# A graph network on one core: TensorE's filler products are removed and their PSUM bank is given to the layers

## The chip, the core and the metric

The kernel runs on one core of one Trainium2 chip. A core has five engines that run their own instruction streams: TensorE (PE in the profile; its weight loads are PEld), VectorE (DVE), ScalarE (ACT), GpSimd (POOL) and the sync engine (SP), which here only issues transfers. TensorE writes its results to PSUM, of which the program uses eight banks of 128 x 512 fp32. The metric is the device time of one execution in microseconds, the median of several runs.

## The reference

Sixteen graphs of 1024 nodes with 64 features each. `adj` holds a weight for each pair of neighbours (about nine a node) and zeros elsewhere. Four layers follow each other, each on the normalised and rectified features, each added to `x`:

```python
h = jnp.maximum(_layernorm(x, axis=-1), 0.0)
x = x + _L0_gnn_ref(h, adj, L0_gnn_W)      # (adj @ h) @ W.T
h = jnp.maximum(_layernorm(x, axis=-1), 0.0)
x = x + _L1_gnn_ref(h, adj, ...)           # two dense layers, adj @ m, then a GRU cell
h = jnp.maximum(_layernorm(x, axis=-1), 0.0)
x = x + _L2_gnn_ref(h, adj, ...)           # K0 h + K1 adj h + K2 (2 adj adj h - h), then dense
h = jnp.maximum(_layernorm(x, axis=-1), 0.0)
x = x + _L3_gnn_ref(h, adj, nodemask, ...) # weighted quantiles over the neighbours, then two dense layers
```

The last layer drops some neighbours of nodes that have more than ten ("dilation"), and takes, for each node and feature, three weighted and interpolated quantiles of the values of the neighbours that are left.

## The kernel before, in words

The program is written by a planner at build time, `Weave` (L311). The work is divided into chains, Python generators that yield one operation at a time. An operation (`Op`, L248) names its engine, the places that it reads and writes, and a reckoned cost (`Line.cost`, L291). `Weave.run` (L415) keeps a reckoned time for each engine, looks at the next operation of each chain, and issues the one that can start first; among those that can start within `SLACK` of it, the chain with the lowest key goes first. The order so found is fixed for each engine (`behind`, L441). Nothing is decided at run time: an engine works through its list, and each instruction waits for the semaphores of what it depends on. The line of nearly all instructions in the profile is therefore that of the helper, L288; gathers have L613, stores L619, scatters L1245.

Each gather on GpSimd is moreover tied to TensorE (`leash`, L394 to L400): it waits for the last of those products that another engine has waited for and that end, by the reckoning, before the gather starts.

The chains are:

- `listing` (L626): loads rows of `adj` and finds each node's neighbours on VectorE (MAX8 and MATCH_REPLACE8 over `key` and `cand`).
- `transposing` (L798): loads blocks of `adj`, turns them on TensorE into the two banks of stock `tp` (`bank<-c,block`), and ScalarE copies them to `AT`. Fifteen `AT` tiles exist.
- `layering` (L1037), twice: two lanes, one for even and one for odd graphs, go through layers 0 to 2 (`layers`, L851). A lane holds one `pay` tile with its graph's features, and takes PSUM banks from stock `fm`, at most two at a time: one while features are multiplied by the adjacency (`bank<-AT,nodes`), a second where the result of the step before is still in use (L921 to L933, L984 to L1008). Products with 64-column weights and 512-column data are two to a pass. At the end a graph's features and lists are stored to HBM (`table`, `rows`).
- `gathering` (L1043): GpSimd fetches, for each graph, 10 x 8 tiles of neighbours' features with indirect DMAs (80 gathers of 128 rows) into one of two `G` tiles. After the 16 graphs come four lists of nodes with many neighbours (`MANY`, L51), picked from all graphs: 22, 28, 48 and 24 gathers.
- `quantiling` (L1072) and `dense` (L1185): VectorE sorts the gathered values with a network of minima and maxima over `G` and `net`, and weighs them (`G<-G,coef`); TensorE sums the weighed cells in a bank of stock `q` (`bank<-G,c`), and goes through the last two dense layers (`bank<-c,yo`, `bank<-of_h,m`, `bank<-m,h`), with ScalarE between them; VectorE masks and adds (`yo<-bank,pay`).

Banks 0 and 1 are stock `tp`, 2 and 3 stock `q`, 4 to 6 stock `fm` (L569 to L571). A stock is a queue: the bank given back longest ago is taken next. Bank 7 belongs to no stock. It takes the products of constants (L565 to L568): a tile of ones, 128 x 128, times ones, 128 x 512, in fp16, whose result nobody reads. When `run` is about to issue an operation on TensorE, and the engine's reckoned idle time before it is over 0.5 us, it first issues as many of these as fill nine tenths of that time at 0.22 us each (L434 to L437). In the built program there are 2705 of them in 223 bursts, each with a weight load of its own. They stand in TensorE's list between the real products, and wait for nothing.

Of the kernel before, what the change touches and what calls it, by code (L numbers as in the profile page):

```python
# [22 lines left out]
P = 128  # L23
# [75 lines left out]
EXTRA = 6 * NT  # L99
BIG = 1e30  # L100
SLACK = 0.1
FILL = 0.9
GATHER = 1.33
RANK = 3.0
SHARE = 3
# [34 lines left out]
def progressions(s):  # L140

    found, top = [], max(s) + 1
    for st in sorted(s):
        found.append((frozenset([st]), (st, 0, 1, 0, 1)))
        for d in range(1, top):
            run = [st]
            while run[-1] + d in s:
                run.append(run[-1] + d)
                found.append((frozenset(run), (st, 0, 1, d, len(run))))
                for e in range(d * (len(run) - 1) + 1, top):  # L150
                    both, k = list(run), 1
                    while all(x + k * e in s for x in run):
                        both += [x + k * e for x in run]
                        k += 1
                        found.append((frozenset(both), (st, e, k, d, len(run))))
    return found
# [56 lines left out]
def fast_constants():  # L213

    k, m = np.arange(P)[:, None], np.arange(P)[None, :]
    r = np.arange(-(NT - 1) * P, N)[None, :]
    half = {
        "keys": ((N - r) * (r != k)),
        "since": (k < m) - 1.0,
        "iota": np.broadcast_to(m, (P, P)),  # L220
        "ordinal": np.broadcast_to(1 + np.arange(LIST)[None, :], (P, LIST)),
    }
    kmax = max(n for _, n in MANY)
    whole = {
        "ident": (k == m),
        "quarter": 0.25 * (k == m),
        "node": P * np.arange(NT)[None, :] + k,
        "shift": np.broadcast_to(P * np.arange(NT)[None, :], (P, NT)),
        "bins": np.broadcast_to(np.array([LONG]), (P, BINS)),
        **{f"place{n}": np.broadcast_to(np.array([order]), (P, len(order))) for n, (_, order) in SORTED.items()},  # L230
        "graph": np.broadcast_to(N * np.arange(GRAPHS)[None, :], (P, GRAPHS)),
        "place": np.broadcast_to(np.arange(kmax)[None, :], (P, kmax)),
        "taus": np.broadcast_to(np.array([TAUS[0], TAUS[1], TAUS[1], TAUS[2]])[None, :], (P, 4)),
    }

    whole["room"] = np.array([[P * sum(t for t, n in MANY if n > many) if many else GRAPHS * N for many in LONG]])
    tables = []
    for parts, dtype in ((half, np.float16), (whole, np.float32)):
        at, cols = {}, 0
        for name, a in parts.items():  # L240
            at[name] = (cols, a.shape[1])
            cols += a.shape[1]
        tables += [np.concatenate([np.broadcast_to(a, (P, a.shape[1])).astype(dtype)
                                   for a in parts.values()], axis=1), at]
    return tables


class Op:  # L248
# [5 lines left out]
    def __init__(self, line, make, writes, reads, cost, later=0.0, after=()):  # L254
        self.line, self.make, self.cost, self.later, self.after = line, make, cost, later, after
        self.writes, self.reads = [place(a) for a in writes], [place(a) for a in reads]
# [54 lines left out]
class Weave:  # L311
# [6 lines left out]
    def __init__(self, tc):  # L318
        self.tc = tc
        self.free, self.past, self.last, self.stocks, self.chains = {}, {}, {}, {}, []  # L320
        self.ends, self.time, self.free_pairs, self.count = {}, 0.0, set(), 0
        self.spare = self.leash = None
        self.awaited, self.made = [], {}

    def stock(self, name, tiles):
# [89 lines left out]
    def run(self):  # L415
        while True:
            before = None
            while before != (before := [(id(c["want"]), id(c["op"])) for c in self.chains]):
                for chain in sorted(self.chains, key=lambda c: c["key"]):
                    if not self.advance(chain):  # L420
                        self.chains.remove(chain)
            heads = [c for c in self.chains if c["op"]]
            if not heads:
                break
            best = {}
            for c in heads:
                op = c["op"]
                c["start"] = max(self.free.get(op.line, 0.0), op.ready)
                best[op.line] = min(best.get(op.line, 1e9), c["start"])
            line = min(best, key=best.get)  # L430
            chain = min((c for c in heads if c["op"].line is line and c["start"] <= best[line] + SLACK),
                        key=lambda c: c["key"])
            op, start = chain["op"], chain["start"]
            if self.spare and line is self.spare[0]:  # L434
                gap = start - self.free.get(line, 0.0)
                for _ in range(int(FILL * gap / self.spare[4]) if gap > 0.5 else 0):
                    self.issue(Op(line, self.spare[1], *self.spare[2:4], self.spare[4]), self.free.get(line, 0.0), ("spare", 0))  # L437
            chain["op"], chain["value"] = None, self.issue(op, start, (chain["gen"].__name__, chain["key"]))
        assert not self.chains, [c["want"] for c in self.chains]

# [14 lines left out]
class Fast:  # L455
# [4 lines left out]
    def __init__(self, tc, half, whole, weights):  # L460
        self.tc, self.nc = tc, tc.nc
        (W0, W1, b1, W2, b2, Wih, bih, Whh, bhh, Wc, K, bc, M1, mb1, M2, mb2) = weights
        nc = self.nc
# [7 lines left out]
        _, at16, _, at32 = fast_constants()  # L471
# [88 lines left out]
        def stock(name, count, shape, dtype=F32):  # L560
            weave.stock(name, [p.tile(shape, dtype, name=f"{name}{i}") for i in range(count)])

        banks = [ps.tile([P, 512], F32, name=f"bank{i}") for i in range(8)]
        self.bank = banks[0]
        busy = banks[7]  # L565
        ones = self.ones16
        weave.spare = (self.T, lambda: nc.tensor.matmul(busy, ones[:, 0:P], ones[:, 0:512], start=True, stop=True),  # L567
                       [busy], [ones], 0.22)  # L568
        weave.stock("tp", banks[0:2])  # L569
        weave.stock("q", banks[2:4])  # L570
        weave.stock("fm", banks[4:7])  # L571


        stock("row", 2, [P, N])
# [1327 lines left out]
```

## Time and profile before

| | |
|---|---|
| median of 3 runs | 2494.44 us (2476.52 to 2508.35) |
| the profiled execution's own time | 2479.22 us |
| its span, first to last instruction | 2477.4 us |
| TensorE's mean granted clock | 0.882 of full speed |
| products (and weight loads) on TensorE | 8704, of which 2705 of constants |
| busy time of the constants' products | 676.4 us |
| gathers on GpSimd | 1402, mean 1.116 us |
| first gather, last gather's end | 152.1 us, 2411.2 us |

A row of the page's groups reads: line, engine, operation, out<-in by the program's names, shapes, count, then busy time and mean ns of one, then the idle time of the engine just before such instructions and what ended it. An fp32 product stands in the trace as two records. A row of the chain gives the share of the span that an engine or a line has on the way back from the last instruction. Rows of stretches give their start and end, the length, each engine's busy time with the number of instructions, the granted clock of TensorE, the share of the DMA engines and GB/s. A row of the timeline gives start, length, engine, line, operation and, in brackets, the idle time before it and what ended it.

### The profile page before, as it was taken

Reading aid. Unit: us, or ns where it says so; the run is one execution under the profiler, and the core shown is the slowest. Engines: PE = TensorE matmul, PEld = TensorE weight load, DVE = VectorE, ACT = ScalarE, POOL = GpSimd, SP = SyncE. Lnnn points to the kernel's source line nnn. Section 1 sums busy time; section 2 is a strip of 40 time slices with the busy share of each in tenths; the row PEclk is TensorE's granted clock in tenths of the full one; section 3 lists DMA queues with packets and bytes.
Section 4 is the critical chain, followed back from the end, with each engine's and each line's share of the span. In section 5 each row is a group of like instructions: output and inputs, shape, how many; then the busy total and the mean of one; then the engine's idle time right before and its main releaser. Section 6 shows DMA issues by size and latency. Waiting matters only on the chain.

```text
span 2477.4 us, 28435 instructions
## 1 busy us (share of the span) xinstructions
PE 2168.9 (88%) x8704; PEld 955.1 (39%) x8704; DVE 1796.3 (73%) x4505; ACT 935.2 (38%) x2714; POOL 1595.6 (64%) x1441
## 2 busy tenths in 40 slices
PE   8999899999898979897988898989898887779857
PEld 3344334343443333434342434342433333334414
DVE  5878687878696878787878877887777484447553
ACT  4444444354444353535353535353534211101000
POOL 1037676767675767676766676776676677777670
PEclk9999898889897989898989898999897887889969
DMA  6345526262626262616252525262522112121110
GB/s 211 111 112 155 115 65 136 57 138 64 121 74 137 56 160 49 149 39 155 56 133 53 139 65 134 60 146 49 140 38 36 23 35 27 23 28 29 23 24 5
DMA packets 265406, 208.68 MB, mean 84 GB/s; under 512 B 78208, under 2 KB 225984, under 8 KB 265248
## 3 DMA queue, kind: packets, MB, share of 16 engines
q1 hardware_dynamic: 218368, 157.32, 23.3%
q0 software_dynamic: 46096, 48.62, 13.0%
q8 instruction: 72, 1.18, 0.2%
q10 hardware_dynamic: 784, 0.86, 0.1%
q14 instruction: 86, 0.70, 0.1%
HBM read 187.51 MB, written 19.17 MB: 83 GB/s over the span
## 4 chain that ended last, share of the span: by engine, by line
PE 61%; DVE 14%; issue 7%; another core or an unknown queue 7%; ACT 7%; DMA 3%; POOL 1%; SPq 0%; ACTq 0%; DVEq 0%; POOLq 0%
PE bank L288 49%; PE bank L567 13%; DVE G L288 5%; DVE net L288 3%; ACT sq L288 2%; DVE cand L288 1%; DMA block<-in_adj 1%; ACT wide L288 1%; DVE hn L288 1%; DMA pay<-in_x 1%; ACT nodes L288 1%; ACT G L288 1%; DVE st L288 1%; DVE pay L288 1%
## 5 line engine op out<-in xcount | busy, mean ns | idle before, releaser
L613 POOL DMA_INDIRECT G<-table,pay x1402 | 1564.9, 1116 | 812.9 <-issue 374.3
L567 PE MATMUL bank<-ones 128*128 128x512 f16 x2705 | 676.4, 399 | 57.4 <-issue 55.7
L288 PE MATMUL bank<-AT,nodes 128*64 128x512 f32 x2048 | 645.9, 650 | 38.8 <-ACT nodes L288 21.2
L567 PEld LDWEIGHTS <-ones 128*128 128x128 f16 x2705 | 267.6, 102 | 412.6 <-issue 162.8
L288 PEld LDWEIGHTS bank<-AT,nodes 128*64 128x64 f32 x2048 | 171.5, 146 | 374.8 <-issue 286.3
L288 ACT ACTIVATE sq<-pay,st 128x64 f32<-128x64 f32 x512 | 177.1, 346 | 130.1 <-DVE st L288 65.5
L288 DVE MAX8 cand<-key 128x8 f16<-128x128 f16 x1024 | 214.4, 279 | 5.7 <-DVE key L288 2.1
L288 ACT ACTIVATE AT<-bank 128x512 f32<-128x512 f32 x256 | 148.3, 591 | 177.5 <-PE bank L288 131.1
L288 ACT ACTIVATE wide<-bank 64x512 f32<-64x512 f32 x128 | 75.6, 591 | 359.8 <-PE bank L288 253.6
L288 PE MATMUL bank<-c,block 128*128 128x128 f32 x976 | 185.7, 313 | 21.1 <-ACT AT L288 9.1
L288 DVE TENSOR_TENSOR G<-G 128x1024 f32<-128x1024 f32 (+7 forms) x215 | 187.2, 903 | 2.6
L288 PEld LDWEIGHTS bank<-c,block 128*128 128x128 f32 x976 | 127.5, 158 | 159.4 <-issue 135.5
L288 DVE SCALAR_TENSOR_TENSOR key<-row,c 128x1024 f16<-128x1024 f32 x124 | 150.2, 1211 | 38.0 <-DMA row<-in_adj 29.3
L288 PE MATMUL bank<-G,c 128*128 128x512 f32 (+3 forms) x382 | 165.0, 571 | 14.0 <-DVE G L288 7.1
L288 ACT ACTIVATE nodes<-pay,off,ri 128x64 f32<-128x64 f32 x384 | 148.8, 430 | 36.1 <-DVE off L288 15.8
L288 DVE TENSOR_TENSOR yo<-bank,pay 128x256 f32<-128x256 f32 (+2 forms) x36 | 14.8, 411 | 181.5 <-PE bank L288 97.6
L288 DVE TENSOR_TENSOR net<-G 128x1024 f32<-128x1024 f32 (+7 forms) x140 | 141.1, 1033 | 1.3
L288 ACT ACTIVATE G<-G,coef 128x64 f32<-128x64 f32 x384 | 93.8, 336 | 96.8 <-DVE coef L288 96.7
L288 DVE TENSOR_TENSOR G<-net 128x512 f32<-128x512 f32 (+12 forms) x123 | 110.2, 939 | 1.2
L288 DVE MAX8 L<-cand 128x8 f16<-128x64 f16 x384 | 87.4, 228 | 29.2 <-remote 9.7
L288 PE MATMUL bank<-wide,wg 64*64 64x512 f32 (+1 forms) x192 | 105.1, 628 | 3.6 <-ACT wide L288 3.4
L288 DVE TENSOR_TENSOR G<-G,net 128x1024 f32<-128x1024 f32 (+5 forms) x113 | 104.4, 960 | 1.4
(176 smaller groups left out, 2238.4 us busy)
## 6 DMA issues: line engine op xcount, KB each, us to landing
row<-in_adj SPq DMA_DIRECT2D x124, 512.0 KB
block<-in_adj SPq DMA_DIRECT2D x122, 512.0 KB
G<-table,pay POOLq DMA_INDIRECT x1402
rows<-pay SPq DMA_DIRECT2D x16, 632.0 KB
G<-in_adj SPq DMA_DIRECT2D x10, 512.0 KB
table<-pay SPq DMA_DIRECT2D x16, 264.0 KB
pay<-in_x SPq DMA_DIRECT2D x16, 256.0 KB
out<-yo SPq DMA_DIRECT2D x16, 256.0 KB
```

The costliest lines, as they stand in the source:

```text
L288: return Op(self, lambda: f(*args, **kwargs), writes, reads, cost, later)
L567: weave.spare = (self.T, lambda: nc.tensor.matmul(busy, ones[:, 0:P], ones[:, 0:512], start=True, stop=True), [busy], [ones], 0.22)
L613: return self.nc.gpsimd.indirect_dma_start(out=out, out_offset=None, in_=table, in_offset=bass.IndirectOffsetOnAxis(ap=at, axis=0))
```

## The change

The block in `run` that issues products of constants goes, with its constant `FILL` and its attribute `spare`. The bank that took their results is the fourth of stock `fm`. Nothing else is changed; the order of the rest is found anew by the same planner.

```diff
-FILL = 0.9
...
-        self.spare = self.leash = None
+        self.leash = None
...
             op, start = chain["op"], chain["start"]
-            if self.spare and line is self.spare[0]:
-                gap = start - self.free.get(line, 0.0)
-                for _ in range(int(FILL * gap / self.spare[4]) if gap > 0.5 else 0):
-                    self.issue(Op(line, self.spare[1], *self.spare[2:4], self.spare[4]), self.free.get(line, 0.0), ("spare", 0))
             chain["op"], chain["value"] = None, self.issue(op, start, (chain["gen"].__name__, chain["key"]))
...
         self.bank = banks[0]
-        busy = banks[7]
-        ones = self.ones16
-        weave.spare = (self.T, lambda: nc.tensor.matmul(busy, ones[:, 0:P], ones[:, 0:512], start=True, stop=True),
-                       [busy], [ones], 0.22)
         weave.stock("tp", banks[0:2])
         weave.stock("q", banks[2:4])
-        weave.stock("fm", banks[4:7])
+        weave.stock("fm", banks[4:8])
```

## The prediction

> **What bounds the kernel now.** I read the page first (busy shares, clock, chain), then the stretches by stage, the waits, and at the end the timeline of the places that they point to. From the page:
>
> ```profile
> PE 2168.9 (88%) x8704; PEld 955.1 (39%) x8704; DVE 1796.3 (73%) x4505; ACT 935.2 (38%) x2714; POOL 1595.6 (64%) x1441
> ...
> PEclk9999898889897989898989898999897887889969
> ...
> PE 61%; DVE 14%; issue 7%; another core or an unknown queue 7%; ACT 7%; DMA 3%; POOL 1%; SPq 0%; ACTq 0%; DVEq 0%; POOLq 0%
> ...
> L613 POOL DMA_INDIRECT G<-table,pay x1402 | 1564.9, 1116 | 812.9 <-issue 374.3
> L567 PE MATMUL bank<-ones 128*128 128x512 f16 x2705 | 676.4, 399 | 57.4 <-issue 55.7
> ```
>
> TensorE is busiest and holds 61% of the chain that ended last, but 676.4 of its 2168.9 us are the products of constants (L567). Real products take 1492 us, 60% of the span. GpSimd's gathers are the second candidate: a gather and its issue cost 1.116 + 0.30 us, so the 80 of one graph 113 us.
>
> By stage (first gather at 152 us, last graph's layers done near 1955), all engines, then the constants alone. Columns: stretch, its length, then PE, PEld, DVE and so on, the granted clock last but two.
>
> ```profile
> 152.00:1955.00 1803.00, 1621.74 (x6424) 713.48 (x6424) 1386.52 (x3546) 801.43 (x2333) 1245.32 (x1120) 0.88 0.42 96
> 1955.00:2477.40 522.40, 409.32 (x1668) 181.69 (x1668) 298.06 (x501) 61.15 (x182) 338.66 (x300) 0.86 0.14 24
> ```
>
> ```profile
> 152.00:1955.00 1803.00, 357.55 (x1400) 138.55 (x1400) 2.23 (x2) 0.88 0.42 96
> 1955.00:2477.40 522.40, 278.08 (x1132) 111.86 (x1132) 0.00 (x0) 0.86 0.14 24
> ```
>
> In the layers' stage real products take 1264 us of 1803, at a mean clock of 0.88. The chain of waits cut to this stage gives 56.6% to real products (1020 us) and 6.9% to constants (124 us). In the tail constants are two thirds of PE's work. The clock in steps of 3 us around one of the longer waits (length, PE busy, clock):
>
> ```profile
> 651.00:654.00 3.00, 2.38 (x8) 1.00 1.19 257
> 654.00:657.00 3.00, 0.00 (x0) 0.80 0.84 172
> 657.00:660.00 3.00, 1.55 (x2) 0.50 1.20 227
> 660.00:663.00 3.00, 3.00 (x13) 0.50 0.82 108
> 666.00:669.00 3.00, 3.00 (x10) 0.50 0.41 64
> 669.00:672.00 3.00, 3.00 (x16) 0.92 0.63 150
> ```
>
> The reader sees what a gap costs: 3 to 4 us without a product, and the clock is halved for 13 us, nine of them full of real work. Stepping through the whole stage so, I count 56 such falls, 433 us at half clock, 7.7 us each. Nearly every 3.4 us with less than about a third of its time in streaming products is followed by a fall, and the clock comes back only after a nearly solid one.
>
> Waits (total, times, longest):
>
> ```profile
> POOL G L613 <- PE bank L288: 161.7, 132, 10.3
> DVE yo L288 <- PE bank L288: 97.6, 23, 23.7
> ```
>
> The gathers wait for real products of PE, since each is tied to the products that the planner puts before it: PE sets the pace of the stage and GpSimd follows close behind. The 23.7 us lies near the end, in the timeline:
>
> ```profile
> 2406.18 2.96 DVE L288 TENSOR_TENSOR G<-G,coef 128x1024 f32<-128x1024 f32 x3
> 2407.49 32.82 PE L567 MATMUL bank<-ones 128*128 128x512 f16 x145 [0.82 <-issue]
> 2439.94 4.29 PEld L288 LDWEIGHTS bank<-G,c 128*128 128x128 f32 x20
> 2450.17 0.42 DVE L288 TENSOR_TENSOR yo<-bank,pay 128x256 f32<-128x256 f32 x1 [23.68 <-PE bank L288]
> ```
>
> The weighted cells are ready at 2409.1, but PE works through constants until 2440.
>
> **What the skill says.** The Trainium skill, "TensorE: Matmul & The Clock Gate", Part 1, "What's actually happening": the array's clock has two states, half and full; an idle window of about 3.4 us brings half, a busy one gives full back. The trace agrees (0.50 and 1.00 above), with one difference: stretches without a gap but thin in work, as at 604 to 614 us, fall too. The same page, "Why this matters for your kernels", advises no PE gap over about 3 us; the constants do that. "PSUM — Partial Sum Buffer", Terms, counts eight banks; the program names eight, and the constants' one is free once they go. "Perfetto Trace Analysis" calls TensorE's end times modelled, so I use start-to-start spacing: 246 constants in 54.16 us, 0.22 us each.
>
> **The change part by part.**
>
> *The fourth bank.* In the built programs the order of TensorE's instructions, constants and bank numbers left out, is the same for the first 2400 of some 3980 rows, and after that only neighbours change places. So the stock of three hardly ever ran empty, and the planner's order barely moves. TensorE's waits on ScalarE fall from 854 to 827, GpSimd's on TensorE from 550 to 544. PE's waits for ScalarE's `wide` are about 1 us each (27.3 us, 27 times), so 27 of them are 27 us at the very most, and most stand where PE waits anyway. Bounds: -20 us to +5 us (a swap that puts a late product first). I take 0.
>
> *Relief: real work no longer queued behind constants.* Upper bound in the stage: constants on the chain, 124 us. Lower bound: I set the first real weight load after each of the 166 bursts against the last semaphore event that it waits for; the delays sum to 75 us, of which 1020/1264 = 0.81 is on the chain, 61 us. I take -100, nearer the top, because the last event is often later than the one needed. Head (0 to 152): 8.4% of the chain is 13 us at most, 7 by the events; I take -9.
>
> *Loss: a colder clock.* The stage's 166 bursts: 25 have 16 products or more (3.4 us and up), 20 have 7 to 15, 121 fewer. I let each long one give one more cold stretch of real work, and every second middle one: 25 + 10 = 35, at 7.7/2 = 3.9 us lost each, 136 us of PE, 0.81 of it on the chain: +110. The short ones I put at nothing: the products around them keep the window full. If that cover fails for one in four, it is 30 stretches more, 95 us on the chain. If half of the long bursts end in a fall already today (constants at half clock are seen: 55 of 345 us), it is 55 us less. Head: 4 long and 2 middle bursts, (4 + 1) x 3.9 x 0.85: +17. In the head the clock is 0.98, so it has most to lose.
>
> *The tail.* From 1955 to 2411 the gathers run nearly without a break, so most constants there lie in real waits, and cost nothing. Three places do. The 23.68 us above goes: the products start at 2409 instead of 2440, take 10 us at full clock and some 18 at half, and are done at 2427, as VectorE gets there (2426.5); about 1 us stays. A gather's wait of 5.85 us at 2334.8, for cells that PE frees late after a burst at 2304 to 2326, goes for 5. The last chain of products (2459 to 2466) is colder: +5. Sum -23.7 + 1 - 5 + 5, about -22. Next late after that is VectorE's network itself.
>
> *Instruction supply.* 5410 of PE's 17408 instructions go. In 2366 to 2407 constants came one in 0.7 us multiples with nothing to wait for. Not priced, bounds 0 to -15.
>
> *Sum.* Head -9 + 17, stage -100 + 110, tail -22: -4 us. Against the execution's own 2479.22 that is 2475. The median shown, 2494.44, is 15 above it; on its footing I say 2490.
>
> **The rivals.**
>
> *Slower: the clock decides.* Real work in the stage is 1264 x 0.88 = 1112 us at full clock. At a mean clock c it takes 1112/c. At c = 0.75 that is 1483, +219, on the chain +177; less relief 100 and tail 22, plus head 10: +65, so 2560. It decides from c = 0.79 down, where 0.81 x (1112/c - 1264) eats the other 114. For it: the thin stretches that fall without any gap. Against: without constants PE's load is 70%, and a half-clocked PE fills its windows with backlog, which brings the clock back.
>
> *Faster: PE regains slack.* Today nine tenths of every reckoned gap are filled, so a PE that is late after a cold stretch cannot catch up, and gathers wait. Full relief 124 + 13, half the loss (55 + 9), tail 22: -95, so 2400. For it: 161.7 us of gathers waiting for PE. Against: the longest such waits (10.3 us at 1944.8, 5.6 at 921) have no or few constants in the 20 us before; PE is full of real work at half clock there.
>
> *The bank does not act,* as above: no time of its own, within the likeliest case.
>
> **How the numbers follow.** Relief and loss balance: 0.46, own range 2445 to 2540. Slower rival 0.30, around 2560; faster 0.24, around 2400. Two per cent (50 us) is about what a measurement of this kernel can tell from no change. So faster 0.24, same 0.46, slower 0.30. The range of 8 in 10 runs from 2425 to 2580: it leaves the outer part of each rival.
>
> **What would show it.** Right: no L567; the clock of the page near 0.75, with the tail lowest; real products' busy time in the layers' stage near 1400 us; VectorE's last wait for PE shorter by some 20 us; PE order as now. Wrong: real busy time near 1264 (no loss), over 1480 (slower rival), or gathers of one graph well under 120 us from first to last (127 now; faster rival).

## The result and the profile after

Changed kernel 2473.92 us (2461.68 to 2483.6), kernel before 2489.37 us on the same chip: ratio 0.9941, 95% interval 0.9923 to 0.9958. The gain on that chip is clear of noise and small, 15 us. The profiled executions have spans of 2477.4 and 2460.4 us.

The lines are those shown of before (there is no row L567 any more), and the instruction queue. The page after, and then the instruction queue's line of before:

```profile
PE 1697.2 (69%) x5999; PEld 760.6 (31%) x5999; DVE 1797.6 (73%) x4505; ACT 935.6 (38%) x2714; POOL 1602.7 (65%) x1441
...
PEclk9768696877787878778787876878867687555555
...
q8 instruction: 51, 0.84, 0.1%
...
PE 51%; DVE 19%; ACT 9%; issue 8%; POOL 6%; DMA 4%; another core or an unknown queue 3%; SPq 1%; DVEq 0%; POOLq 0%; ACTq 0%
...
L604 POOL DMA_INDIRECT G<-table,pay x1402 | 1572.4, 1122 | 811.1 <-issue 365.4
```

```profile
q8 instruction: 72, 1.18, 0.2%
```

TensorE works 472 us less and runs colder: the mean clock falls from 0.882 to 0.74, and the last six slices of forty are all near half. The two stretches of the prediction, bounded by the same gathers as there (so they start and end later), and two waits:

```profile
163.00:1974.00 1811.00, 1419.63 (x5025) 624.96 (x5025) 1387.80 (x3545) 801.86 (x2333) 1250.61 (x1120) 0.77 0.42 96
1974.00:2460.40 486.40, 161.28 (x538) 83.50 (x538) 298.02 (x501) 61.07 (x182) 340.48 (x300) 0.59 0.14 26
```

```profile
POOL G L604 <- PE bank L287: 175.6, 146, 9.3
DVE yo L287 <- PE bank L287: 67.8, 18, 11.1
```

Real products of the layers' stage are busy for 1420 us instead of 1264. (The 1264 is a difference, which gives time that real products share with constants to the constants; counted by themselves they took 1300 us.) By the trace, the gathers wait somewhat longer for them, and VectorE's masking of results shorter. Its wait of 23.7 us is gone. The timeline of that place:

```profile
2411.95 2.96 DVE L287 TENSOR_TENSOR G<-G,coef 128x1024 f32<-128x1024 f32 x3
...
2413.32 7.12 PE L287 MATMUL bank<-G,c 128*128 128x256 f32 x20 [67.83 <-DVE G L287]
...
2430.93 0.42 DVE L287 TENSOR_TENSOR yo<-bank,pay 128x256 f32<-128x256 f32 x1
```

TensorE sits idle when the weighted cells come, takes them at once, and VectorE finds the sums ready.

Cut at four places of the gathers' row (first gather; first gather of graph 14; last gather of graph 15; last gather of the lists; end), the span is

| piece | before | after | change |
|---|---|---|---|
| head | 152.1 | 163.0 | +10.9 |
| stage | 1803.0 | 1811.0 | +8.0 |
| last two graphs' gathers | 245.1 | 239.2 | -5.9 |
| lists | 211.0 | 202.5 | -8.5 |
| rest | 66.2 | 44.7 | -21.5 |

The loss stands ahead (head and stage, 19 us) and the gain behind (36 us).

### The profile page after: what moved, and what is told of

Same layout as the page of the kernel before. It is cut to its first block, busy times and chain, and to the rows that moved or that the text cites. A ratio compares the mean times of both kernels' runs of the same rounds, so it can differ in the third digit from the quotient of the medians.

```text
span 2460.4 us, 23041 instructions
## 1 busy us (share of the span) xinstructions
PE 1697.2 (69%) x5999; PEld 760.6 (31%) x5999; DVE 1797.6 (73%) x4505; ACT 935.6 (38%) x2714; POOL 1602.7 (65%) x1441
## 4 chain that ended last, share of the span: by engine, by line
PE 51%; DVE 19%; ACT 9%; issue 8%; POOL 6%; DMA 4%; another core or an unknown queue 3%; SPq 1%; DVEq 0%; POOLq 0%; ACTq 0%
PE bank L287 51%; DVE G L287 6%; POOL G L604 5%; DVE net L287 3%; ACT sq L287 3%; DMA block<-in_adj 2%; DVE cand L287 1%; ACT wide L287 1%; DVE hn L287 1%; DMA pay<-in_x 1%; DVE pay L287 1%; DVE st L287 1%; DVE key L287 1%; ACT AT L287 1%
## 5 line engine op out<-in xcount | busy, mean ns | idle before, releaser
L287 PE MATMUL bank<-AT,nodes 128*64 128x512 f32 x2048 | 688.1, 694 | 160.1 <-ACT nodes L287 86.4
L287 PE MATMUL bank<-G,c 128*128 128x512 f32 (+3 forms) x382 | 186.1, 640 | 246.5 <-DVE G L287 240.0
L287 PEld LDWEIGHTS bank<-AT,nodes 128*64 128x64 f32 x2048 | 183.4, 156 | 519.2 <-issue 337.2
L287 PE MATMUL bank<-c,block 128*128 128x128 f32 x976 | 215.6, 350 | 102.8 <-ACT AT L287 57.8
L287 PEld LDWEIGHTS bank<-c,block 128*128 128x128 f32 x976 | 145.3, 178 | 256.8 <-issue 167.3
L287 PEld LDWEIGHTS bank<-G,c 128*128 128x128 f32 x382 | 81.0, 248 | 313.1 <-DVE G L287 182.0
L287 DVE SCALAR_TENSOR_TENSOR G<-bad,G 128x1024 f32<-128x1024 f32 (+3 forms) x89 | 102.5, 1203 | 0.3
```

Of the source, the lines that this page charges most:

```text
L287: return Op(self, lambda: f(*args, **kwargs), writes, reads, cost, later)
```

## The experiments

The chip isn't always the same one. The kernel before takes 2489 us where the result was taken, 2485 where the second four kernels ran, 2295 where the first four and the last four ran. Ratios are always to the kernel before on the same chip. "Slower chip" and "faster chip" below mean no more than this: each set ran once, on one chip, and what makes the two kinds differ isn't known. Their traces differ as well: on the slower chips they hold about half as many semaphore events (17,434 in before, 34,267 in e11_slivers, which has the same instructions). Instructions are recorded alike on both. So who ended a wait, and the chain built from it, is less sure in the traces of the slower chips, and the main readings below rest on the starts of instructions that wait for nothing.

**Where do the constants pay?** A burst is a row of constants between two real products. Bursts only in one part of the kernel, by a condition on the graphs stored so far; the first version has no constants and keeps three banks.

```diff
-            if self.spare and line is self.spare[0]:
+            if self.spare and line is self.spare[0] and self.filling():
...
+        self.weave.filling = lambda: len(self.paid) < GRAPHS - 1    # e2_until_layers_end
+        self.weave.filling = lambda: len(self.paid) == 0            # e3_head_only
+        self.weave.filling = lambda: len(self.paid) >= GRAPHS - 1   # e4_tail_only
```

> No products of constants, but the layers keep three banks and the eighth stays unused. If the gain comes of the constants alone (relief against a colder clock), this is the changed kernel again: ratio to the kernel before 0.992 to 0.997, clock 0.74, first gather near 163 us. If the fourth bank carries the gain, it is lost here: ratio 1.000 to 1.006.

> Constants as in the kernel before until the last but one graph's layers are stored, none after (1508 of 2705 stay). If constants keep the clock up in head and stage and only stand in the way in the tail: first gather at 152 us, the stage as before, from the last gather's end to the last instruction about 45 us and not 66, in all 25 to 36 us less than before, ratio 0.985 to 0.990, better than the changed kernel. If constants hinder the layers as well, it is no better than the changed kernel: ratio 0.994 or more.

> Constants only until the first graph's layers are stored (121 of 2705). If the head alone pays for the lost clock: first gather near 152 us, 11 us before the changed kernel's, the rest like the changed kernel's: ratio 0.988 to 0.992. If the later start of the changed kernel is made good anyway by waits further on, ratio 0.993 to 0.996.

> Constants only from where the last but one graph's layers are stored (1197 of 2705). If the tail holds the gain, this has head and stage of the changed kernel and the tail of the kernel before: first gather near 163, VectorE's long wait near the end (20 us and more) back, ratio 1.003 to 1.010. If the gain is in the stage: ratio 0.990 to 0.996.

Measured, before 2294.93 us:

| | time | ratio (95%) | head | stage | rest |
|---|---|---|---|---|---|
| e1_three_banks | 2352.38 | 1.0242 (1.0200 to 1.0285) | 164.3 | 1714.6 | 471.2 |
| e2_until_layers_end | 2298.08 | 1.0005 (0.9987 to 1.0022) | 158.3 | 1665.9 | 473.2 |
| e3_head_only | 2339.94 | 1.0166 (1.0128 to 1.0204) | 155.5 | 1723.3 | 473.5 |
| e4_tail_only | 2355.27 | 1.0253 (1.0219 to 1.0287) | 163.1 | 1720.8 | 473.4 |

Pieces are of the profiled execution (that of e3_head_only took 2354 us). Here removing the constants costs 2.4%: 49 to 57 us in the stage, 5 to 9 in the head. The changed kernel itself, with its fourth bank, was not run here. In the tail the constants neither help nor hurt: with and without them the rest takes 471 to 474 us, and in e4_tail_only VectorE's long wait near the end isn't there (8.4 us at most). No expectation had foreseen that. So what the change gained in the tail, 36 us on the chip of the result, isn't there on this one.

The stage with and without constants, first e2_until_layers_end (all work, then the constants alone), then e1_three_banks:

```profile
158.30:1824.20 1665.90, 1542.02 (x6359) 680.01 (x6357) 1380.43 (x3538) 798.92 (x2332) 1264.57 (x1121) 0.91 0.49 104
```

```profile
158.30:1824.20 1665.90, 329.74 (x1332) 129.42 (x1332) 0.91 0.49 104
```

```profile
164.30:1878.90 1714.60, 1377.41 (x5027) 605.20 (x5027) 1384.02 (x3543) 800.07 (x2333) 1267.64 (x1121) 0.80 0.47 101
```

Real products take 1542 - 330 = 1212 us with constants and 1377 without: the colder clock costs 165 us of PE, as on the chip of the result (1264 to 1420, 156). Counted by themselves they rise by 129 (from 1249) and 120 (from 1300). The clock's price is thus much the same on both. What differs is then what the constants themselves cost.

**What the constants cost on the slower chip.** The trace of before has an answer that I had looked at and not priced. Its timeline of TensorE in the tail:

```profile
2376.41 0.59 PE L567 MATMUL bank<-ones 128*128 128x512 f16 x1 [3.61 <-issue]
2379.21 0.59 PE L567 MATMUL bank<-ones 128*128 128x512 f16 x1 [2.21 <-issue]
2381.34 1.33 PE L567 MATMUL bank<-ones 128*128 128x512 f16 x2 [1.54 <-issue]
2384.87 0.58 PE L567 MATMUL bank<-ones 128*128 128x512 f16 x1 [2.21 <-issue]
2386.27 0.58 PE L567 MATMUL bank<-ones 128*128 128x512 f16 x1 [0.82 <-issue]
```

Constants wait for nothing, and yet they start 1.4, 2.1, 2.8 us apart, multiples of 0.7, where 0.216 us is the rule. Of the 2482 steps from one constant to the next, 51 are over 0.6 us. They last 81 us together, 70 more than at 0.216: 12 us of that in the stage, 58 in the tail. Most are near multiples of 0.7. The burst ahead of the 23.7 us wait, 261 constants, takes 95 us; in e4_tail_only, on the faster chip, the same burst takes 56.5. In e2_until_layers_end and e4_tail_only not one step of 1330 and 1152 is over 0.6 us. Real products don't show it: in the traces of before and after, none of the some 4,600 that wait for nothing starts over 0.6 us after the end of the one ahead.

Theory B, formed here: on some chips TensorE's instructions come now and then one at a time, 0.7 us or a multiple apart; the constants are 5410 of its 17408 (each a weight load and a product), so dropping them takes away the shortage where they were dense. Theory A, the prediction's: queue and clock alone. They part over the number of instructions at the same occupancy. I made the constants long (fp32, a quarter of the number) and narrow (twice the number):

```diff
-  weave.spare = (self.T, lambda: nc.tensor.matmul(busy, ones[:, 0:P], ones[:, 0:512], start=True, stop=True),
-                 [busy], [ones], 0.22)
+  # e7_wide
+  weave.spare = (self.T, lambda: nc.tensor.matmul(busy.rearrange("p (a c) -> p a c", a=2), ones.bitcast(F32)[:, 0:P],
+                 ones.bitcast(F32)[:, None, 0:256].to_broadcast([P, 2, 256]), start=True, stop=True),
+                 [busy], [ones], 0.88)
+  # e8_narrow
+  weave.spare = (self.T, lambda: nc.tensor.matmul(busy[:, 0:256], ones[:, 0:P], ones[:, 0:256], start=True, stop=True),
+                 [busy], [ones], 0.11)
```

> The changed kernel itself, a second time. The first four experiments ran on a chip on which the kernel before takes 2295 us and not 2489. Theory A (colder clock against relief of the queue behind the constants, alike on every chip): ratio 0.994 on any chip. Theory B (on the chip of the result TensorE is now and then short of instructions, in steps of 0.7 us, and most of that falls in the constants; the change gains by dropping 5410 of its instructions): 0.994 where before takes about 2490, and about 1.02 where it takes about 2295, since there only the colder clock is left.

> No constants and three banks for the layers: what the fourth bank is worth beside e5_changed_again, on the same chip. The prediction: from 20 us slower to 5 us faster without it. Theory A and B give the same here: within 0.5% of e5_changed_again. The rival that the bank is what the change gains by: 1% or more slower than e5_changed_again.

> The constants as fp32 products of four times the length: 576 instead of 2705, about 507 us of TensorE's gaps filled instead of 595, with far fewer instructions for the same occupancy. Theory A: the clock stays within 0.03 of before, and a product in work keeps the next real one waiting longer (up to 0.9 us instead of 0.2), so 0 to 1.5% slower than before on any chip. Theory B: where before takes about 2490, 1 to 2.5% faster than before and faster than the changed kernel; where it takes about 2295, as theory A.

> The constants with half the columns: 5540 of them at about 0.11 us, the same time filled with twice the instructions. Theory A: within 0.5% of before on any chip. Theory B: where before takes about 2490, 2 to 4% slower than before, with more of the steps of 0.7 us in the constants; where it takes about 2295, within 0.5%, unless the weight loads of 0.05 to 0.1 us no longer hide behind products so short.

Measured, before 2484.75 us:

| | time | ratio (95%) | constants' instructions | steps over normal, sum |
|---|---|---|---|---|
| e5_changed_again | 2481.17 | 0.9977 (0.9954 to 1.0001) | 0 | |
| e6_three_banks_again | 2476.54 | 0.9964 (0.9939 to 0.9988) | 0 | |
| e7_wide | 2465.68 | 0.9897 (0.9869 to 0.9924) | 2304 | 15, 13 us |
| before | 2484.75 | 1 | 5410 | 51, 70 us (trace of the result) |
| e8_narrow | 2578.56 | 1.0377 (1.0328 to 1.0426) | 11080 | 132, 155 us |

(Long steps: over 0.6 us, for the wide ones over 0.9, since each of a wide product's two records takes 0.43 at full clock and 0.85 at half.) The wide and the narrow ones came as theory B said; theory A's "0 to 1.5% slower" and "within 0.5%" both fail. The changed kernel came back smaller than either theory had it: 0.9977, an interval that reaches 1 and leaves out 0.994. Narrow constants start 0.109 us apart at full clock, so their weight loads hide, and their occupancy is nearly the same (5540 x 0.109 = 604 us, 2705 x 0.216 = 584 us). They were not run on a faster chip, so a price of their own that isn't the long steps stands untested; but the long steps grew by 85 us and the time by 94. Their page, and 10 us of their timeline:

```profile
PE 65%; issue 10%; DVE 9%; ACT 6%; another core or an unknown queue 6%; DMA 3%; POOL 1%; SPq 0%; DVEq 0%; ACTq 0%; POOLq 0%
PE bank L288 47%; PE bank L567 18%; DVE G L288 3%; ACT sq L288 2%; ACT wide L288 1%; DVE net L288 1%; POOL G L613 1%; DMA pay<-in_x 1%; DVE hn L288 1%; DVE cand L288 1%; DMA block<-in_adj 1%; ACT G L288 1%; DVE row L288 1%; DVE st L288 1%
...
L567 PE MATMUL bank<-ones 128*128 128x256 f16 x5540 | 732.9, 287 | 136.7 <-issue 131.6
```

```profile
2461.80 0.37 PE L567 MATMUL bank<-ones 128*128 128x256 f16 x1 [2.42 <-issue]
2464.61 0.37 PE L567 MATMUL bank<-ones 128*128 128x256 f16 x1 [2.44 <-issue]
2467.41 0.37 PE L567 MATMUL bank<-ones 128*128 128x256 f16 x1 [2.44 <-issue]
2470.21 0.37 PE L567 MATMUL bank<-ones 128*128 128x256 f16 x1 [2.43 <-issue]
```

Here a product of 0.11 us starts every 2.8 us; constants hold 18% of the chain. The page of e7_wide:

```profile
PEclk9889897979798978888998888898979697989888
...
PE bank L288 45%; DVE G L288 7%; POOL G L614 5%; DVE net L288 4%; ACT sq L288 2%; DVE cand L288 2%; PE bank L567 2%; DVE hn L288 1%; DMA row<-in_adj 1%; DMA block<-in_adj 1%; DVE key L288 1%; ACT wide L288 1%; DVE pay L288 1%; DMA pay<-in_x 1%
...
L567 PE MATMUL bank<-ones 128*128 128x512 f32 x1152 | 555.4, 627 | 8.5 <-issue 7.2
```

The clock is kept (0.868), constants hold 2% of the chain instead of 13%, and TensorE's idle time ahead of them falls from 57.4 to 8.5 us. This version beats both kernels on that chip.

The bank: e6_three_banks_again and e5_changed_again differ by less than their intervals, so the fourth bank brings nothing that shows here.

**Is it the number, the occupancy or the arithmetic?** The last four ran where before takes 2295.4 us, so that the first two could not test what I had meant them for.

```diff
-  weave.spare = (self.T, lambda: nc.tensor.matmul(busy, ones[:, 0:P], ones[:, 0:512], start=True, stop=True),
+  # e11_slivers
+  weave.spare = (self.T, lambda: nc.tensor.matmul(busy[:, 0:8], ones[:, 0:P], ones[:, 0:8], start=True, stop=True),
+  # e12_one_row
+  weave.spare = (self.T, lambda: nc.tensor.matmul(busy, ones[0:1, 0:P], ones[0:1, 0:512], start=True, stop=True),
```

> Constants until 15 graphs are stored, none after (1508 of the 2705), once more, for the tail on a chip where before takes about 2485. Theory B (a short supply of TensorE's instructions): in before the tail, from the last layer on, takes 522 us and holds 58 us of long steps between constants; here it takes about 484 as in the changed kernel, the stage stays near 1803: 30 to 40 us faster than before, ratio about 0.985, and faster than the changed kernel. Theory A (queue and clock alone): the tail gains the predicted 22 us, ratio 0.991. Where before takes about 2295: 1.00, as e2_until_layers_end had.

> The wide fp32 constants, and those until 15 graphs are stored only (294 products). Theory B: the stage of e7_wide (1795 us) and the tail of the changed kernel: some 2455 us where before takes 2485, ratio 0.985 to 0.99, the best of all versions together with e9_until_again. Theory A: no better than e7_wide, since the tail loses its clock. Where before takes about 2295: 1.00 to 1.01.

> The constants cut to 8 columns, in the same places and in the same number: as many instructions, almost no occupancy, so a real product has next to nothing to wait behind. Theory A: the clock falls to about 0.75 and the queue is gone, so the time is that of the changed kernel, ratio 0.994 to 1.00. Theory B: the stalls stay in part and the clock is lost as well: ratio 1.01 to 1.03 where before takes about 2485. Where it takes about 2295: 1.02 to 1.03, as without constants.

> The constants with one row in place of 128, same columns, number and places: TensorE is as long in work, on a 128th of the arithmetic. If the clock follows time in work: 0.88 and ratio 1.00. If it follows the arithmetic: about 0.75, and the time is worse than before by the clock's price with no stall taken away, ratio 1.02 to 1.03. Theory A and B agree here; it says what the granted clock follows.

| | time | ratio (95%) | clock |
|---|---|---|---|
| e9_until_again | 2294.73 | 0.9996 (0.9981 to 1.0012) | 0.847 |
| e10_wide_until | 2301.49 | 1.0018 (0.9998 to 1.0037) | 0.837 |
| e11_slivers | 2344.97 | 1.0209 (1.0174 to 1.0243) | 0.762 |
| e12_one_row | 2739.27 | 1.1933 (1.1893 to 1.1974) | 0.723 |

The first two repeat the tail's nothing, and are a control: where no long steps are (one of 1.0 us among the wide ones), wide constants gain nothing over the usual ones. The slivers (8 columns) are a second: they follow each other at 0.026 us, none over 0.6, so dense instructions alone don't bring the long steps about; the chip has to be of the other kind.

The last was a surprise. One row in place of 128 leaves the columns, and the steps between constants are 0.215 us at full clock as before. Page of e12_one_row:

```profile
PE 2684.2 (98%) x8704; PEld 1075.0 (39%) x8704; DVE 1796.3 (66%) x4505; ACT 937.0 (34%) x2714; POOL 1584.6 (58%) x1441
...
PEclk9768685777787886978777777787867755555555
...
L567 PE MATMUL bank<-ones 1*128 1x512 f16 x2705 | 1043.9, 562 | 0.4 <-DVE wg L535 0.4
```

TensorE is in work for 98% of the span, and the clock is lower than with no constants at all; in the tail it stays at half. The Trainium skill, "TensorE: Matmul & The Clock Gate", "What's actually happening", says that the clock follows how busy TensorE has recently been. This run narrows that: time in work with one row of 128 did not hold it. Row counts in between were not run. I had expected 1.02 to 1.03 for this case and left out the other half: at half clock the constants last 0.427 us where the planner reckons 0.22, overfill every gap, and real products queue behind them. e11_slivers loses the clock too (0.762) and has 69 us of constant-to-constant steps where this has 930: the 394 us between them are, nearly all, what a filled queue costs. The gathers' waits for real products say the same; e11_slivers has 138.1 us of them, e12_one_row:

```profile
POOL G L613 <- PE bank L288: 440.6, 219, 52.7
```

## Why the prediction came out as it did

The forecast was 2490 with a sum of -4; the spans moved by -17, the medians by -15. The likeliest case is the one that came, but one term of the sum was mis-sized, and which chip it is decides on it. That the sum came near all the same isn't the merit of its parts: relief and tail were read off this chip's trace, and so hold late constants without naming them. On the faster chip the same -4 would have missed the sign.

- *Fourth bank, 0.* Right: 0.9964 with three, 0.9977 with four, on one chip.
- *Colder clock, +136 us of PE in the stage.* Right in size: +156 by the prediction's difference (1264 to 1420), +120 with real products counted by themselves. Wrong in form: my "35 cold stretches more at 3.9" are 9 more (65 instead of 56), but each now lasts 12.2 us on average, not 7.7. The tail's clock is the lowest, as said. The rule behind it comes out of the trace of before: cut into windows of 3.413 us, the shortest stretch at one clock that it has, with each product counted at its columns' time (0.216 us for 512 in fp16, 0.43 for each record of fp32, both twice that at half clock), 27 of 27 full-clock windows of the stage with under 0.35 of their time in products are followed by half clock, 24 of 56 with 0.35 to 0.65, 5 of 318 fuller ones; after half clock, full clock follows 45 of 46 windows with over 0.85. One bound was added up wrongly: half of the 25 long bursts is 40 us less, not 55 (that is half of all 35 stretches).
- *Relief, -100 in the stage.* The net of +10 came as +8.0. With 0.81 x (120 to 156) = 97 to 126 of loss, relief is -89 to -118 by subtraction. On the faster chip it is 0.81 x (129 to 165) - 49 = 55 to 85: some of what I took for a queue behind constants was perhaps constants that came late themselves (12 us of long steps stand in the stage). The split is an estimate; only the net is measured. The lower bound of 61 us was none: it was counted from semaphore events, of which that trace lacks about half.
- *Head, +8.* Measured +10.9.
- *Tail, -22.* Measured -36. The place of the 23.7 us wait was right, its cause only half. The real products stood behind the burst because the burst took 95 us; on the faster chip, with bursts of the same lengths in the same order, the tail gains nothing by losing its constants (471 to 474 us either way).
- *Instruction supply, "Not priced, bounds 0 to -15".* This is the step that failed: a cost seen in the trace and put at 15 us at most. Removing the constants leaves 2352.4 us on one chip and 2476.5 on another (three banks on both), 124 apart; with constants it is 2294.9 and 2484.8, 190 apart. So 66 us (give or take 12, by the intervals) of what the constants cost there, and don't cost elsewhere, go with them. The long steps counted in the trace, 70 us, fit in sum. By place they fit in the tail: 58 us of them, and 36 us gained where the faster chip gains none. Those 36 us alone decide the sign; without them the change would have lost some 20 us (an estimate). In head and stage, where removing constants costs 19 to 38 us on the slower chips and 55 on the faster, 12 us of long steps are too few to explain the rest; profiles of e5_changed_again and e6_three_banks_again differ by 15 us there, and the cause of that part stays open.
- *Rivals.* The slower one came true on the faster chip (+2.4%), with 0.80 in the stage where it put the deciding point at 0.79. On the chip of the result the stage stands at 0.77, below that point, and the time still fell, since the long steps outweighed it. The faster one didn't come: graphs 4 to 14 still take 122 to 130 us from first to last gather.

The Trainium skill, "Runtime: NRT & Kernel Launch", "Instruction fetch mechanics", says that instructions are fetched in blocks of 256, and that crossing one is mostly hidden. The trace agrees on the block: the instruction queue's packets fall from 72 to 51, 21 blocks or 5376 instructions, for 5410 removed. The long steps don't speak against "hidden": in the trace of before none of the 51 overlaps a packet of that queue. The longest run of them, 2364 to 2407 us, lies between packets at 2346 and 2412. So fetching a block isn't what they wait for, as far as the trace tells.

What stays open: why some chips have these steps, and what the 124 us are that remain between the chips without constants. The experiments show that the steps go with the number of constants; "short supply" is a name for it. The rival that they leave is the recording: the chips with the long steps are those whose traces lack half of the semaphore events, and the more instructions TensorE has, the fewer events are left (19,181 at most without constants, 17,434 before, 17,067 with narrow ones). So the profiler may be what holds TensorE up there, and without it the kernel might not have the steps. No run here tests that. The missing events also make waits that no one seems to have ended. Waits of the kernel before, where "remote" means that the profile knows no releaser:

```profile
ACT wide L288 <- remote: 90.6, 11, 14.8
ACT of_h L288 <- remote: 54.6, 8, 13.1
```

No trace of a faster chip has one such wait on ScalarE, and after the change `wide` still has 82.9 us of them. They can't be told from waits whose event wasn't recorded, so they say nothing of ScalarE. The tail without constants, and the wide ones in the layers only, were not measured on a slower chip, so that the tail's 36 us are late constants is argued from the trace and not tested alone.

## What to carry to other kernels

Filler for TensorE's clock has two prices here: real products that queue behind it, and its instructions (the bank that it held brought nothing elsewhere). It paid in the clock with 128 rows and 256 or 512 columns, and not with one row or with 8 columns. Fill a given time with few long products rather than many short ones: that gained 1% on a slower chip and lost nothing that shows on a faster one. A step on the timeline that waits for nothing and lasts a multiple of what it should is to be priced like any other wait: here it decided the sign, and taking the constants out was -0.6% on one chip, -0.2% on a second and, with three banks, +2.4% on a third. A forecast read off one chip's trace holds for that chip.

## What the runs showed of the hardware that was not expected

- The same kernel takes 2295 us on some chips and 2485 to 2489 on others, 8% apart; without constants 2352 and 2477, 5% apart.
- In the traces of the slower ones constants start in stretches at steps of 0.7 us or a multiple: 51 steps over 0.6 us before, 132 with twice the instructions, none among fp16 constants on the faster ones.
- The same traces hold 17,067 to 19,181 semaphore events, those of the faster ones 34,267 to 34,386.
- One-row products of 512 columns take 0.215 us at full clock, as those with 128 rows, and did not hold the clock: 0.723 at 98% in work.
- Products with 8 columns, each with its own 128-row weight load, follow each other at 0.026 us. The Trainium skill, "TensorE: Matmul & The Clock Gate", "Wait — 56ns, not 53.3ns?", gives a floor of about 25 ns from start to start; the trace agrees.
